# A depthwise convolution moved from VectorE to TensorE, and a longer ring of row tiles, in the first scan of a fused state-space and attention kernel

## The chip, the core and the metric

The kernel runs on one core of a Trainium2 chip. The core has a matrix engine (TensorE, PE in the profile; its weight loads are PEld), a vector engine (VectorE, DVE), an activation engine (ScalarE, ACT), a general engine (GpSimd, POOL) and a queue engine (SyncE, SP) that here issues most of the transfers. The engines run their own instruction streams in order and wait for each other with semaphores. 16 DMA engines carry the transfers. The metric is the device time of one execution in microseconds.

## What is computed

The input x is 32 sequences of 256 tokens with 256 channels. A state-space layer turns it into y, two attention and feed-forward layers follow, and x is added at the end. All is float32. The part that the change touches is the front of the state-space layer (cut to what matters):

```
xr, gate = jnp.split(x @ W_in.T, 2, axis=-1)          # 512 channels each
xr = xr + t_emb[:, None, :]
xc = conv_general_dilated(xr.transpose(0, 2, 1), W_conv, (1,), [(3, 0)],
                          feature_group_count=512) + b_conv   # 4 taps, each channel by itself
xc = silu(xc).transpose(0, 2, 1)
xn = (xc - mean) / sqrt(var + 1e-05) * ln_g + ln_b
Bm, Cm, dt = split(xn @ W_xproj.T, 3, axis=-1)        # 16 states
dt = tanh(dt @ W_dt.T + b_dt) * 0.01
Ad = 1.0 + dt * -tanh(A_log);  Bd = Bm * min(norm(xn), 1.0)
h = clip(h * Ad + Bd * xt, -10, 10);  yt = Ct . h     # a scan over the 256 tokens
y = (ys + D * xn) * silu(gate) @ W_out.T
```

Each token's state h is 16 states by 512 channels per sequence. The convolution is depthwise: an output channel is the sum of four shifted copies of the same input channel, each times a weight of that channel.

## The kernel before

The 32 sequences are four groups of eight (GB). A group's scan holds 8 sequences x 16 states on the 128 partitions and 512 channels along them, so one token of a group is one VectorE instruction of 128x512 (`step`, L718): 256 steps per group, 1024 in all. A token's row of xn has to stand on all 16 states of its sequence, times that state's factor. For most tokens a DMA reads the row from DRAM (tensor xnd) and spreads it over the partitions (`load_rows`, L687, tile xrep); ScalarE multiplies it by the factor (`scale_row`, L708); the step adds it to h. In the first group two tokens of every eight come another way: `load_skip` loads a block of 16 rows (tile xq, L747), and TensorE spreads a row by a product (`spread_rows`, L695, tile bx), which ScalarE scales into a tile of the same ring. Row tiles come from a ring of six (pool xp).

The work of a scan is written as an agenda. Slot s is the step of token s; everything else has a slot relative to it, and a chunk of 32 tokens (CH) starts at slot s0. For the first group (`alone`) the chunk's x is loaded at s0-43; `project` (L401) makes the four blocks of 128 channels from s0-40 on, every second slot; then `conv_in` (s0-38 + 2 ch) puts the 3 tokens carried over from the last chunk (GpSimd, L471 and L473) and the projection plus condition (VectorE, L474) into tile xr, and GpSimd begins the convolution in tile acc with tap 0 and the bias (L480). `conv_taps` one slot later adds taps 1 to 3 on VectorE (L491), and `conv_th` one slot after that takes the Silu on ScalarE (L501). The tiles xr and acc have two buffers each. `raw_sums` (s0-27, L520) and `norm_turn` (s0-26 and s0-22, L550) use the result on TensorE; statistics, scaling and the affine follow, and `norm_out` (s0-17 and s0-13, L593) writes 128 rows each to xnd. `load_skip` reads blocks back at s0-9 and s0+7; `load_rows` of token t stands at slot s0+t-6, and `scale_row` at s0+t-2. Outputs are read from h by TensorE (`read_out`, L730), in groups of four tokens, and gated, turned and projected (L781 to L832). The state tiles h have eight buffers.

During the first scan TensorE also makes the projections of the three other groups, in 48 units (`ahead_project`, L428, 16 records of 256 columns for every two units), which go to DRAM and come back later. The other groups' scans are then interleaved with attention and feed-forward of the groups before; attention starts at slot 274. These groups compute the convolution on GpSimd and VectorE in all versions, with Tanh in place of Silu.

SP's queue holds, in order: row loads, loads of x (L457, L417), blocks xq, writes of xnd, writes of projected tiles (L444), and loads of weights. An instruction in it that waits for a tile to come free holds all that stand behind it. All eight PSUM banks are one pool (psw, tag w) for every kind of product. The order within a slot is first the agenda of the state work and then that of loads and products; from this order and its own estimate of times the framework's planner lays out each engine's stream, and an instruction may be taken ahead of others that wait. Where a tile is given to a new owner, the instruction that first writes it waits for the last owner's users.

The function `program` holds two versions of everything; the data choose the one with `exact` false.

Of the kernel before, what the change touches and what calls it, by code (L numbers as in the profile page):

```python
# [10 lines left out]
FP = mybir.dt.float32  # L11
# [62 lines left out]
def kernel(  # L74
# [149 lines left out]
    def program(ctx, exact):  # L224
# [154 lines left out]
        def group_scan(g):  # L379
# [82 lines left out]
            def conv_in(c, ch):  # L462
                if ch == 0:
                    ck[c]["carry"] = sm.tile(
                        [P, NC_, GB, TAPS - 1], FP, tag="carry", name="carry"
                    )
                    ck[c]["xc"] = sp.tile([P, NC_, GB * CH], FP, tag="xc", name="xc")
                ps = ck[c].pop(("ps", ch))
                xr = sp.tile([P, GB, TAPS - 1 + CH], FP, tag="xr", name="xr", bufs=2)
                if c == 0:  # L470
                    nc.gpsimd.memset(xr[:, :, 0 : TAPS - 1], 0.0)  # L471
                else:
                    nc.gpsimd.tensor_copy(xr[:, :, 0 : TAPS - 1], ck[c - 1]["carry"][:, ch])  # L473
                nc.vector.tensor_add(  # L474
                    xr[:, :, TAPS - 1 :],
                    ps.rearrange("p (b t) -> p b t", b=GB),
                    bc(cond_sb[:, ch, b0 : b0 + GB], 2, CH),
                )
                acc = sp.tile([P, GB, CH], FP, tag="acc", name="acc", bufs=2)
                nc.gpsimd.tensor_scalar(  # L480
                    acc, xr[:, :, 0:CH], wc_sb[:, ch, 0:1], bconv_sb[:, ch : ch + 1],
                    ALU.mult, ALU.add,
                )
                if c < NCH - 1:
                    nc.gpsimd.tensor_copy(ck[c]["carry"][:, ch], xr[:, :, CH:])
                ck[c]["xr", ch] = xr, acc

            def conv_taps(c, ch):
                xr, acc = ck[c]["xr", ch]
# [6 lines left out]
            def conv_th(c, ch):  # L496
                acc = ck[c]["xr", ch][1]
                if alone:

                    ck[c].pop(("xr", ch))  # L500
                    nc.scalar.activation(  # L501
                        ck[c]["xc"][:, ch], acc.rearrange("p b t -> p (b t)"), AF.Silu
                    )
                    return
                th = sp.tile([P, GB * CH], FP, tag="th", name="th", bufs=2)
                nc.scalar.activation(th, acc.rearrange("p b t -> p (b t)"), AF.Tanh, scale=0.5)
                ck[c]["th", ch] = th
# [173 lines left out]
            def by_tensor(t):  # L681
                return alone and t % (2 * NQ) < XR

            def load_rows(c, t):
                xr = xp.tile([P, DI], FP, tag="xrep", name="xrep")
                ck[c]["rep", t] = xr
                nc.sync.dma_start(out=xr, in_=bc(rows(c)[:, t, :], 0, NS))  # L687

# [14 lines left out]

            def scale_row(c, t):
                if by_tensor(t):
                    ck[c]["rep", t] = xp.tile([P, DI], FP, tag="xrep", name="xrep")
                bx = ck[c]["rep", t]
                scaled = nc.scalar.activation(  # L708
                    bx, ck[c].pop(("bx", t), bx), AF.Copy, scale=ck[c]["beta"][:, t : t + 1]
# [140 lines left out]
            rep_w = []  # L850
            at(-1, start)
            if alone:
                at(-30, spread_weights)
                constants(at)
            for c in range(NCH):
# [2 lines left out]
            for c in range(NCH):  # L858
# [7 lines left out]
                    at(s + 11, skip, c, hb)  # L866
                for ch in range(NC_):
                    at(s0 - 38 + 2 * ch, conv_in, c, ch)
                    at(s0 - 37 + 2 * ch, conv_taps, c, ch)
                    at(s0 - 36 + 2 * ch, conv_th, c, ch)  # L870
                    if not alone:
                        at(s0 - 35 + 2 * ch, conv_out, c, ch)
# [24 lines left out]
            for c in range(NCH):  # L897
                s0 = c * CH
                at(s0 - 43 if alone else s0 + 6, load_x, c)
                if alone:  # L900
                    for ch in range(NC_):
                        at(s0 - 40 + 2 * ch, project, c, ch)
                else:
                    for i in range(2):
                        at(s0 - 44 + 2 * i, load_projected, c, i)
# [5 lines left out]
                at(s0 - 8, figures_out, c)  # L911
                for t in range(CH):
                    if not by_tensor(t):
                        at(s0 + t - 6, load_rows, c, t)
                    if by_tensor(t) and t % XR == 0:
                        at(s0 + t - 4, spread_rows, c, t)
                    at(s0 + t - 2, scale_row, c, t)
# [777 lines left out]
```

## Time and profile before

| | us |
|---|---|
| median of 3 runs | 3543.61 (3540.46 to 3543.66) |
| the profiled execution | 3553.66 |
| its span, first to last instruction | 3551.9 |
| busy in the span: TensorE, VectorE, ScalarE, GpSimd | 3441.7, 2605.5, 2037.4, 1620.7 |
| first scan, first step's start to last step's end | 59.2 to 448.7 |

A group line of the profile reads: line of the program, engine, operation, output tile <- input tiles, partitions x elements, count | busy us, mean ns of one | idle time of the engine just before them, and what ended it. A wait line reads: who waited for whom, total us, times, longest. A timeline line reads: start, duration, engine, line, operation, count, and in brackets the idle time before it. Matmuls are pipelined and their ends are modelled, so the time from one start to the next says more of TensorE's pace than its busy time does. One product of float32 operands appears as two records.

### The profile page before, as it was taken

What the parts mean: (1) busy time and instruction counts of PE and PEld (TensorE: products, weight loads), DVE (VectorE), ACT (ScalarE), POOL (GpSimd) and SP (SyncE); (2) the same over time, 40 slices, a digit from 0 to 9 for tenths busy, and PEclk for the clock granted to TensorE, in tenths of its full rate; (3) what the DMA queues carried; (4) which work ended last, traced back from release to release, by engine and by line L of the source; (5) the groups of instructions that cost most, each with busy time, mean ns of one, the idle gap of its engine ahead of it and who ended that gap; (6) DMA issues with size and microseconds to landing.
All of it is one profiled execution on the core that took longest, in us unless ns stands there. A gap on an engine that the chain in (4) does not pass through costs nothing.

```text
span 3551.9 us, 57690 instructions
## 1 busy us (share of the span) xinstructions
PE 3441.7 (97%) x20220; PEld 2263.7 (64%) x20220; DVE 2605.5 (73%) x5049; ACT 2037.4 (57%) x3663; POOL 1620.7 (46%) x1587
## 2 busy tenths in 40 slices
PE   7999989999999999999999999999999999999999
PEld 5445335666666666666666666666666777777777
DVE  4888898877878777877787778787777545555563
ACT  3666656656666656666566656666666444444442
POOL 4433455544545445544454556454443333333441
PEclk8999999999999999999999999999999999999999
DMA  6788765534454555544454445544444212011111
GB/s 183 211 219 217 200 174 153 135 113 134 125 143 138 150 144 150 139 121 126 123 144 131 139 147 146 145 115 129 124 138 118 63 37 62 13 31 35 37 28 38
DMA packets 487199, 436.72 MB, mean 123 GB/s; under 512 B 247155, under 2 KB 326516, under 8 KB 486772
## 3 DMA queue, kind: packets, MB, share of 16 engines
q1 hardware_dynamic: 402450, 420.94, 42.0%
q10 hardware_dynamic: 84450, 12.01, 2.1%
q8 instruction: 162, 2.65, 0.3%
q14 instruction: 137, 1.12, 0.1%
HBM read 384.06 MB, written 47.19 MB: 121 GB/s over the span
## 4 chain that ended last, share of the span: by engine, by line
PE 64%; DVE 16%; DMA 7%; ACT 5%; POOL 4%; issue 3%; SPq 1%; ACTq 0%; DVEq 0%; POOLq 0%
PE ps_qkv L991 13%; PE pa L1402 13%; PE po_f L1429 6%; DVE h L718 6%; DMA xrep<-xnd 5%; PE y L730 5%; PE ps_wo L1047 5%; PE ov L1282 4%; PE ps_in L401 3%; PE ps_out L810 3%; PE sc L1227 3%; PE tr_qk L1036 2%; PE rs L1264 2%; ACT xrep L708 2%; DVE acc L491 2%
## 5 line engine op out<-in xcount | busy, mean ns | idle before, releaser
L718 DVE CUSTOM_DVE_ANT_0 h<-h,xrep,lim 128x512 f32<-128x512 f32 x1024 | 931.9, 910 | 215.1 <-ACT xrep L708 166.5
L708 ACT ACTIVATE xrep<-xrep,beta 128x512 f32<-128x512 f32 x960 | 672.5, 720 | 315.7 <-DMA xrep<-xnd 202.4
L991 PE MATMUL ps_qkv<-qkv,res 128*128 128x512 f32 x1536 | 715.2, 601 | 17.2 <-DVE ag L1420 7.2
L1402 PE MATMUL pa<-hT,w 128*128 128x256 f32 (+1 forms) x2816 | 674.5, 382 | 5.4 <-DVE zT L801 5.1
L1402 PEld LDWEIGHTS pa<-hT,w 128*128 128x128 f32 (+1 forms) x2816 | 517.6, 189 | 145.1 <-issue 38.0
L1015 POOL TENSOR_TENSOR rot<-rot,swp 128x512 f32<-128x512 f32 x256 | 349.0, 1363 | 543.7 <-DVE swp L1012 513.0
L991 PEld LDWEIGHTS ps_qkv<-qkv,res 128*128 128x128 f32 x1536 | 282.2, 191 | 299.8 <-issue 242.2
L1021 POOL TENSOR_TENSOR rn<-ss,neg_half 128x8 f32<-128x8 f32 x256 | 461.0, 1801 | 0.0
L1420 DVE SCALAR_TENSOR_TENSOR ag<-pa,b_sb,ag 128x256 f32<-128x256 f32 x320 | 151.9, 475 | 280.0 <-ACT ag L1413 279.7
L730 PE MATMUL y<-h,ly 128*32 128x512 f32 x2048 | 335.8, 606 | 9.8 <-DVE h L718 9.2
L1429 PE MATMUL po_f<-ag,w 128*128 128x256 f32 x1280 | 305.7, 386 | 1.4 <-DVE fo L1440 0.6
L1354 POOL TENSOR_TENSOR rstd<-ve,neg_half 128x2 f32<-128x2 f32 x64 | 46.1, 720 | 555.9 <-DVE ve L1352 555.9
L1429 PEld LDWEIGHTS po_f<-ag,w 128*128 128x128 f32 x1280 | 235.3, 190 | 64.8 <-DVE xc L511 11.7
L1413 ACT ACTIVATE ag<-pa,b_sb 128x256 f32<-128x256 f32 x320 | 149.9, 469 | 217.8 <-PE pa L1402 215.7
L1004 ACT ACTIVATE sq<-ps_qkv,tiny 128x512 f32<-128x512 f32 x256 | 172.4, 685 | 172.2 <-PE ps_qkv L991 143.8
L1047 PE MATMUL ps_wo<-oT,wo 128*128 128x256 f32 x1024 | 236.2, 385 | 14.2 <-DVE oT L1322 11.2
L1047 PEld LDWEIGHTS ps_wo<-oT,wo 128*128 128x128 f32 x1024 | 196.6, 193 | 45.5 <-issue 9.9
L491 DVE SCALAR_TENSOR_TENSOR acc<-xr,wc_sb,acc 128x256 f32<-128x256 f32 x384 | 188.6, 523 | 46.4 <-POOL acc L480 45.9
L1012 DVE TENSOR_TENSOR swp<-ps_qkv,rs_sb 128x256 f32<-128x256 f32 x512 | 191.8, 416 | 29.8 <-POOL rot L1015 29.6
L1007 DVE TENSOR_TENSOR rot<-ps_qkv,rc_sb 128x512 f32<-128x512 f32 x256 | 173.8, 679 | 45.8 <-ACT sq L1004 45.6
L1239 ACT ACTIVATE pT<-sc 128x512 f32<-128x512 f32 x384 | 202.1, 603 | 7.3 <-PE sc L1227 5.5
L1027 DVE SCALAR_TENSOR_TENSOR rot<-rn,rot 128x512 f32<-128x512 f32 x256 | 196.1, 804 | 5.0 <-POOL rn L1021 4.7
(161 smaller groups left out, 5306.9 us busy)
## 6 DMA issues: line engine op xcount, KB each, us to landing
xrep<-xnd SPq DMA_DIRECT2D x960, 256.0 KB
rb<-inv SPq DMA_DIRECT2D x128, 256.0 KB
xnd<-xn SPq DMA_DIRECT2D x64, 256.0 KB
qkv<-in_wqkv_dram SPq DMA_DIRECT2D x24, 512.0 KB
ahead<-xs_a SPq DMA_DIRECT2D x48, 256.0 KB
xp<-ahead SPq DMA_DIRECT2D x48, 256.0 KB
xd<-xnd SPq DMA_DIRECT2D x192, 64.0 KB
w<-in_w_dram SPq DMA_DIRECT2D x80, 128.0 KB
```

The lines of the kernel that those rows point to most:

```text
L491: nc.vector.scalar_tensor_tensor(acc, xr[:, :, k : k + CH], wc_sb[:, ch, k : k + 1], acc, ALU.mult, ALU.add,)
L708: scaled = nc.scalar.activation(bx, ck[c].pop(("bx", t), bx), AF.Copy, scale=ck[c]["beta"][:, t : t + 1])
L718: nc.vector._custom_dve(TENSOR_ADD_SAT, out=h_new, in0=state["h"], in1=bx, s0=ck[c]["lim"][:, 0, t : t + 1], s1=ck[c]["lim"][:, 1, t : t + 1],
L730: nc.tensor.matmul(ck[c]["y", hb][32 * q : 32 * q + 32, :], ly[hb % 2][:, 32 * t : 32 * t + 32], ck[c].pop(("h", hb * TB + t)), start=(i = ...
L991: nc.tensor.matmul(ps, res[b][:, k, t0 : t0 + W], wt["qkv", a][:, k], start=(k == 0), stop=(k == KM - 1),)
L1015: nc.gpsimd.tensor_add(rot, rot, swp)
L1021: nc.gpsimd.tensor_tensor(rn, ss, neg_half, ALU.pow)
L1027: nc.vector.scalar_tensor_tensor(rot, bc(rn, 2, DH), 1e12, rot, ALU.min, ALU.mult)
L1047: nc.tensor.matmul(po[:, d], wt["wo", 0][:, c, d * P : (d + 1) * P], oT[:, c, :], start=(c == 0), stop=(c == NC_ - 1),)
L1239: nc.scalar.activation(p, banks[r], AF.Exp)
L1402: nc.tensor.matmul(dst[x], wt["w1", m][:, k, x], self.h[:, k], start=(k == 0), stop=(k == KM - 1),)
L1429: nc.tensor.matmul(self.po[:, d], wt["w2", 0][:, m, d * P : (d + 1) * P], self.ag[m], start=(m == 0), stop=(m == len(MCH) - 1),)
```

## The change

In the first scan the convolution's taps become TensorE products: the input block xr, shifted by k tokens, times a 128x128 matrix that has tap k's weights on its diagonal, four products summed in a PSUM bank; ScalarE adds the bias in the Silu and reads the bank. The 16 diagonals are made once, by ScalarE from the identity, in tiles that the attention uses later (tags oT, hn, hT). The ring of row tiles of the first scan grows from six to ten; the four new ones are tiles of the attention (tags qT, kT, rb, v). Its row loads are issued eight slots ahead of the step instead of six.

```diff
                     bc(cond_sb[:, ch, b0 : b0 + GB], 2, CH),
                 )
-                acc = sp.tile([P, GB, CH], FP, tag="acc", name="acc", bufs=2)
-                nc.gpsimd.tensor_scalar(
-                    acc, xr[:, :, 0:CH], wc_sb[:, ch, 0:1], bconv_sb[:, ch : ch + 1],
-                    ALU.mult, ALU.add,
-                )
+                acc = None
+                if not alone:
+                    acc = sp.tile([P, GB, CH], FP, tag="acc", name="acc", bufs=2)
+                    nc.gpsimd.tensor_scalar(
+                        acc, xr[:, :, 0:CH], wc_sb[:, ch, 0:1], bconv_sb[:, ch : ch + 1],
+                        ALU.mult, ALU.add,
+                    )
                 if c < NCH - 1:
                     nc.gpsimd.tensor_copy(ck[c]["carry"][:, ch], xr[:, :, CH:])
                 ck[c]["xr", ch] = xr, acc
+
+            def taps_diagonal(ch):
+                if ch == 0:
+                    t = ap_.tile([P, 2, TAPS, P], FP, tag="oT", name="taps", bufs=1)
+                    state["taps", 0], state["taps", 1] = t[:, 0], t[:, 1]
+                elif ch > 1:
+                    state["taps", ch] = ap_.tile(
+                        [P, TAPS, P], FP, tag=("hn", "hT")[ch - 2], name="taps", bufs=1
+                    )
+                for k in range(TAPS):
+                    nc.scalar.activation(
+                        state["taps", ch][:, k], ident, AF.Copy, scale=wc_sb[:, ch, k : k + 1]
+                    )
+
+            def conv_products(c, ch):
+                xr, _ = ck[c]["xr", ch]
+                ps = bank(ps_w, "w", "cv")[:, 0 : GB * CH]
+                for k in range(TAPS):
+                    nc.tensor.matmul(
+                        ps.rearrange("p (b t) -> p b t", b=GB),
+                        state["taps", ch][:, k],
+                        xr[:, :, k : k + CH],
+                        start=(k == 0),
+                        stop=(k == TAPS - 1),
+                    )
+                ck[c]["xr", ch] = xr, ps
...
                     nc.scalar.activation(
-                        ck[c]["xc"][:, ch], acc.rearrange("p b t -> p (b t)"), AF.Silu
+                        ck[c]["xc"][:, ch], acc, AF.Silu, bias=bconv_sb[:, ch : ch + 1]
                     )
...
+            def row_tile():
+
+                n = state["rows"] = (state.get("rows", -1) + 1) % (6 if exact else 10)
+                if not alone or n < 6:
+                    return xp.tile([P, DI], FP, tag="xrep", name="xrep")
+                tag = ("qT", "kT", "rb", "v")[n - 6]
+                t = ap_.tile(
+                    [P, 2, DI], FP, tag=tag, name="xrep", bufs=2 if tag == "v" else 1
+                )
+                return t[:, 0]
+
             def load_rows(c, t):
-                xr = xp.tile([P, DI], FP, tag="xrep", name="xrep")
+                xr = row_tile()
...
             def scale_row(c, t):
                 if by_tensor(t):
-                    ck[c]["rep", t] = xp.tile([P, DI], FP, tag="xrep", name="xrep")
+                    ck[c]["rep", t] = row_tile()
...
             if alone:
+                for ch in range(NC_):
+                    at(-41 + ch, taps_diagonal, ch)
...
                     at(s0 - 38 + 2 * ch, conv_in, c, ch)
-                    at(s0 - 37 + 2 * ch, conv_taps, c, ch)
+                    if not alone:
+                        at(s0 - 37 + 2 * ch, conv_taps, c, ch)
                     at(s0 - 36 + 2 * ch, conv_th, c, ch)
...
                     for ch in range(NC_):
                         at(s0 - 40 + 2 * ch, project, c, ch)
+                        at(s0 - 37 + 2 * ch, conv_products, c, ch)
...
-                        at(s0 + t - 6, load_rows, c, t)
+                        at(s0 + t - (8 if alone and not exact else 6), load_rows, c, t)
```

## The prediction

> **What bounds the kernel now.** I read the page's head, then windows of one chunk each, the groups and waits of the first scan, and the timelines of TensorE and of SP's queue.
>
> ```profile
> span 3551.9 us, 57690 instructions
> ...
> PE 3441.7 (97%) x20220; PEld 2263.7 (64%) x20220; DVE 2605.5 (73%) x5049; ACT 2037.4 (57%) x3663; POOL 1620.7 (46%) x1587
> ```
> TensorE bounds the whole, but the change touches only the first scan. Its steps (L718) start at 59.2 us and end at 448.7: 389.5 us for 8 chunks of 32 slots, 48.7 us each, 1.52 per slot. Windows of a chunk (PE, PEld, DVE, ACT, POOL busy; clock, DMA share, GB/s):
> ```profile
> 160.00:209.00 49.00, 46.23 (x216) 24.46 (x215) 42.78 (x75) 31.99 (x61) 19.15 (x26) 1.00 0.80 218
> 209.00:258.00 49.00, 45.60 (x189) 24.86 (x192) 41.33 (x74) 29.81 (x55) 18.27 (x25) 0.93 0.84 220
> ...
> 402.00:449.00 47.00, 41.54 (x135) 13.43 (x134) 41.36 (x80) 28.23 (x50) 22.19 (x28) 1.00 0.63 175
> ```
> VectorE has 42 of 49 us, and no engine is full. The groups between 150 and 400 us (5.1 chunks) show what the taps cost:
> ```profile
> L718 DVE CUSTOM_DVE_ANT_0 h<-h,xrep,lim 128x512 f32<-128x512 f32 x164 | 156.6, 955 | 11.5 <-ACT xrep L708 3.5 <-DVE h L718 2.0 <-PE y L730 1.1
> ...
> L491 DVE SCALAR_TENSOR_TENSOR acc<-xr,wc_sb,acc 128x256 f32<-128x256 f32 x65 | 32.8, 505 | 6.2 <-POOL acc L480 6.2
> L480 POOL TENSOR_SCALAR acc<-xr,wc_sb,bconv_sb 128x256 f32<-128x256 f32 x22 | 21.5, 978 | 45.3 <-DVE xr L474 39.4 <-ACT xrep L708 4.0 <-ACT xs_a L439 1.9
> ```
> The waits of the same 250 us (total, times, longest): ScalarE waits for rows, SP's queue for a free row tile (a load needs the step six rows back), and TensorE for the blocks of rows that queue up behind those loads.
> ```profile
> DVE ad L650 <- ACT ad L645: 7.2, 5, 2.0
> ...
> ACT xrep L708 <- DMA xrep<-xnd: 52.6, 44, 3.5
> ...
> PE bx L695 <- DMA xq<-xnd: 7.7, 5, 1.9
> ...
> SPq L687 <- DVE h L718: 35.7, 44, 2.9
> ```
> SP's timeline shows it at a chunk's end: the block is issued at 244.31, after 2.86 us in which a row load waited, and TensorE then idles until 249.67, its first products slow.
> ```profile
> 240.15 2.86 SPq L687 DMA_DIRECT2D xrep<-xnd  x1
> ...
> 244.31 2.64 SPq L747 DMA_DIRECT2D xq<-xnd  x4
> ```
> TensorE's timeline gives its pace, from start to start, since its busy time counts tails:
> ```profile
> 227.82 1.07 PE L730 MATMUL y<-h,ly 128*32 128x512 f32 x8
> ...
> 230.65 1.89 PE L401 MATMUL ps_in<-xg,w_in_sb 128*128 128x256 f32 x8
> ...
> 236.30 1.89 PE L428 MATMUL ps_a<-xa,w_in_sb 128*128 128x256 f32 x8
> 238.12 1.13 PE L695 MATMUL bx<-xq,rep_w 32*128 32x512 f32 x4
> ...
> 249.67 3.11 PE L695 MATMUL bx<-xq,rep_w 32*128 32x512 f32 x4 [2.54 <-ACT xrep L708]
> ```
> Eight records of 256 columns take 1.82 us (236.30 to 238.12), 0.2275 each; each product is two records (16 projections a chunk by the code, 152 records in 5.1 chunks).
>
> **The change, part by part.**
>
> *Taps off VectorE and GpSimd.* Per chunk 12 L491 go. They are 0.505 us each by the group; started back to back in the timeline they advance it by about 0.43, so 5.2 us. The 4 L480 of 0.98 us go too, with VectorE's wait for them, 6.2 / 5.1 = 1.2 us. VectorE falls from 42 to about 37 us of busy time.
>
> *Products onto TensorE.* 4 blocks x 4 taps x 2 records = 32 records x 0.2275 = 7.3 us per chunk. What TensorE already issues per chunk: 104 records of 256 columns (48 L428, 32 L401, 16 L810, 8 L520) 23.7; 16 of L695, four per 1.06 us, 4.2; 64 of L730, eight per 1.00 us, 8.0; 16 transposes 2.0; L620 0.5. Sum 38.4, so 10.3 of the 48.7 us are waits or half clock. After: 45.7. Idle time covers the products, but hardly any is left: **TensorE becomes the bound of the first scan at about 45.7 us per chunk.** The other limits lie lower: VectorE 37, ScalarE 32, DMA 217 GB/s x 48.7 us at a share of 0.80, so 39 us at a share of 1.
>
> *Ring of ten, loads eight slots ahead.* The load now needs the step ten allocations back, two slots done by plan. SP's 35.7 us of waiting for steps should mostly go, and with it what is queued behind: writes of xnd, blocks xq, ahead, xg. Each load is issued two slots (3 us) earlier, with unchanged count and bytes. The first rows of a chunk must follow the write of xnd, but load_skip, one slot earlier in SP's queue, waits for that write already: nothing added. Unless the late block's waits go (7.7 / 5.1 = 1.5 us per chunk, and about as much in half clock), TensorE's 10.3 us of slack isn't usable, so the two parts need each other.
>
> *New waits.* xr has two buffers, now released by TensorE instead of VectorE; conv_in's add stands in VectorE's queue ahead of steps, and a late product holds the steps. Bounds: 0, or three adds a chunk each behind one block's products (1.8 us), 5.5 us. The plan has three slots between, so I take 0.6 with the other residual waits. One more PSUM bank: between 0 and the one bank-like wait shown (L695 behind ACT xrep, 2.5 us in 250), 0.5 per chunk; I take 0. The Silu now reads PSUM; PSUM readers of that size (L474, 0.42) and this row (0.41) differ by nothing.
>
> *Borrowed tiles.* Attention's first use is at slot 274, after the last row's step at 255: 0. Without that cover the first projections would wait a step, 1.5 us.
>
> *Startup.* 16 diagonals on ScalarE: rows of 0.31 (128x32) and 0.41 (128x256) bound them at 5 to 6.6 us; ScalarE is idle 7.3 us there before its first Silu at 17.2, so 0, or 6.6 if they hold the first Silu. Chunk 0's 32 records replace taps that end at 24.9. TensorE's pace there:
> ```profile
> 9.68 5.46 PE L401 MATMUL ps_in<-xg,w_in_sb 128*128 128x256 f32 x12 [9.68 <-DMA xg<-in_xT_dram]
> ...
> 18.02 2.00 PE L428 MATMUL ps_a<-xa,w_in_sb 128*128 128x256 f32 x8
> ...
> 29.66 3.76 PE L428 MATMUL ps_a<-xa,w_in_sb 128*128 128x256 f32 x8
> ```
> At 18 us a record takes 0.24, before 15 and at 30 us 0.45. 32 records are 7.3 to 14.6 us, against about 5 idle us between 15 and 25. [...]
>
> [...]
>
> *Sum.* Chunk with products: 45.7 + 0.6 = 46.3, 2.4 less, in six chunks: 14.4. The last two have no products, only the ring: their floor is VectorE's 41.4 of 47; of 5.6 us I take a third, 1.8 each: 3.6. Startup 0. The attention that follows is TensorE's and unchanged: 0. Together 18 us. The profiled execution took 3553.7 (span 3551.9), 10 above the median of 3543.6; against the median: **3526**. Own range: 3517 to 3536.
>
> **Rivals.**
> - *TensorE too full, slower.* The 10.3 us of waits don't vanish when work is added. If half stay, a chunk takes 45.7 + 5.2 = 50.9: 2.2 more in six, 13; less 3.6; with startup up to 7: 3553 to 3560. It decides from 3.0 us of residual waits per chunk. For: TensorE's order is fixed, and it waits on h, xq and rhs. Against: these waits come from late rows.
> - *Rows are limited by the transfers.* Then the ring only queues them longer: 0 to 1 us per chunk, 3536 to 3550. For: 5 us windows reach a DMA share of 1. Against: 0.8 on the mean, and SP waiting for steps.
> - *More.* At 0.216 per record (chain of waits: eight in 1.73) the floor is 44; with 4.3 in six chunks, 4 in two and 5 at startup: 3505.
> - *The planner's order undoes it* (products late, rows as before): within the second rival.
>
> **How the numbers follow.** No change means within 0.2%, 7 us, about what a measurement tells. Forecast 0.50, more 0.14: faster 0.64. Transfers or order 0.14: same. TensorE 0.22: slower. The range reaches past 3505 by startup's bound, to 3497, and to 3557 in the slower rival.
>
> **What would show it.** Right: chunks of 46 to 47 us, no L491 and L480 ahead of the second group's convolution, VectorE near 37 per chunk, SP's waits for h nearly gone, ACT's for rows halved, TensorE's start-to-start sum 45 to 46 per chunk at full clock. Wrong: chunks over 48.7; VectorE's L474 waiting for the products; L695 still waiting for xq; the DMA share at 1; a first step later than 59.2 us; or any change in time after 449 us, which nothing here explains.

## The result and the profile after

The changed kernel took 3579.21 us (median of 5, 3576.81 to 3583.29) against 3543.61 for the kernel before: a ratio of 1.010, 95% interval 1.0088 to 1.0112. It is **36 us slower**. The forecast was 3526 us, so the sign was wrong. The rival that had TensorE too full had the sign but gave 3553 to 3560.

The profiled execution took 3582.63 us. These are the span and the busy times of its page.

```profile
span 3580.8 us, 58077 instructions
...
PE 3464.5 (97%) x20476; PEld 2294.1 (64%) x20476; DVE 2552.2 (71%) x4953; ACT 2045.0 (57%) x3679; POOL 1601.5 (45%) x1555
```

The step is now L757 and the row load L726. The first scan runs from 55.1 to 475.7 us, 420.6 us of steps. Before it was 389.5, and 391.7 in another profiled execution of the kernel before (3544.93 us). After the last step of the first scan 3105.2 us remain, against 3103.2 and 3104.1. So 29 to 31 us of the 36 come from the steps of the first scan, and nothing from what follows it. By chunk, from first step to first step (the last one to the first step of the second group), in us:

| chunk | 0 | 1 | 2 | 3 | 4 | 5 | 6 | 7 |
|---|---|---|---|---|---|---|---|---|
| before | 52.0 | 48.8 | 48.9 | 49.9 | 48.4 | 48.2 | 47.5 | 46.6 |
| after | 53.1 | 51.0 | 53.1 | 51.5 | 54.2 | 57.4 | 54.8 | 46.2 |

"A chunk" below is the mean of chunks 1 to 5: 48.8 before (48.9 in the other execution), 53.4 after. These are the windows of the changed kernel over the stretches shown of before (PE, PEld, DVE, ACT, POOL busy; clock, DMA share, GB/s).

```profile
160.00:209.00 49.00, 43.40 (x217) 26.48 (x216) 30.97 (x54) 28.33 (x53) 14.26 (x17) 1.00 0.73 198
209.00:258.00 49.00, 44.88 (x223) 27.13 (x222) 34.34 (x58) 30.95 (x57) 16.46 (x21) 0.97 0.71 191
402.00:449.00 47.00, 42.93 (x155) 16.42 (x156) 38.85 (x75) 25.27 (x46) 19.41 (x26) 0.96 0.61 188
```

VectorE is relieved, 31 and 34 of 49 us where it had 43 and 41, and TensorE, ScalarE and GpSimd are busy for no more of the time than before. The DMA share fell from 0.80 and 0.84 to 0.73 and 0.71. So no engine has taken over as one that is always at work: they wait for each other. Two groups of 150 to 400 us, the step and the new products:

```profile
L757 DVE CUSTOM_DVE_ANT_0 h<-h,xrep,lim 128x512 f32<-128x512 f32 x149 | 130.1, 873 | 61.5 <-ACT xrep L747 40.8 <-PE y L769 13.0 <-DVE h L757 1.2
...
L507 PE MATMUL cv<-xr,taps 128*128 128x256 f32 x160 | 40.1, 393 | 5.6 <-DVE xr L474 4.3 <-DVE ad L678 1.3
```
The waits of the same 250 us on ScalarE and TensorE (total, times, longest):
```profile
ACT xrep L747 <- DMA xrep<-xnd: 79.6, 44, 6.3
...
PE ps_raw L548 <- ACT xc L529: 5.4, 4, 2.2
...
PE cv L507 <- DVE xr L474: 4.3, 3, 2.3
```
And those of SP's queue:
```profile
SPq L726 <- DVE h L757: 36.8, 45, 3.7
SPq L444 <- ACT xs_a L439: 31.6, 14, 5.2
SPq L621 <- POOL xn L617: 24.8, 9, 4.2
```

The steps idle 61.5 us (11.5 before), ScalarE waits 79.6 us for rows (52.6 before), and SP still waits as long for steps (36.8; 35.7 before). Which rows the steps wait for is told by the tile bx, the rows that TensorE spreads. Among those who waited for an instruction on bx that ran in these 250 us (total, times), the step stands as follows, first in the changed kernel, then in the kernel before:
```profile
  DVE h L757: 44.7, 14
```
```profile
  DVE h L718: 0.2, 1
```
In the other execution of the kernel before it is 1.4 us. So the steps' new waits for ScalarE are for TensorE's rows, not for loaded ones. In the changed kernel ScalarE scales, in chunks 1 to 5, 4.0 loaded rows of later tokens on the mean ahead of the first TensorE row of eight tokens (0.1 before), and any of them can make it wait for a transfer.

The timelines at 269 to 280 us show how one wait makes the next. SP's queue:

```profile
272.60 1.04 SPq L726 DMA_DIRECT2D xrep<-xnd  x1
278.89 0.34 SPq L444 DMA_DIRECT2D ahead<-xs_a  x1
279.29 4.21 SPq L726 DMA_DIRECT2D xrep<-xnd  x5
```
ScalarE:
```profile
275.97 0.72 ACT L747 ACTIVATE xrep<-xrep,beta 128x512 f32<-128x512 f32 x1 [3.08 <-DMA xrep<-xnd]
277.31 0.72 ACT L747 ACTIVATE xrep<-xrep,beta 128x512 f32<-128x512 f32 x1 [0.62 <-DMA xrep<-xnd]
277.94 0.46 ACT L529 ACTIVATE xc<-cv,bconv_sb 128x256 f32<-128x256 f32 x1
278.30 0.57 ACT L439 COPY xs_a<-ps_a 128x512 f32<-128x512 f32 x1
278.76 1.28 ACT L747 ACTIVATE xrep<-bx,beta 128x512 f32<-128x512 f32 x2
```
TensorE:
```profile
269.02 2.00 PE L507 MATMUL cv<-xr,taps 128*128 128x256 f32 x8
270.86 1.89 PE L428 MATMUL ps_a<-xa,w_in_sb 128*128 128x256 f32 x8
272.67 1.13 PE L734 MATMUL bx<-xq,rep_w 32*128 32x512 f32 x4
273.73 1.06 PE L769 MATMUL y<-h,ly 128*32 128x512 f32 x8
274.73 1.51 PE L548 MATMUL ps_raw<-xc,wx_sb 128*64 128x256 f32 x6
278.45 0.65 PE L548 MATMUL ps_raw<-xc,wx_sb 128*64 128x256 f32 x2 [2.21 <-ACT xc L529]
```
VectorE:
```profile
279.50 0.81 DVE L757 CUSTOM_DVE_ANT_0 h<-h,xrep,lim 128x512 f32<-128x512 f32 x1 [6.09 <-ACT xrep L747]
```

The last convolution product is done by 270.9. Its Silu (L529) stands in ScalarE's queue behind the scaling of rows that arrive late, so it ends at 278.4, and TensorE waits 2.21 us for it. The copy of projected tiles (L439) stands behind it, SP's put of that copy waits until 278.89, and five row loads wait behind the put. VectorE's next step waits 6.09 us meanwhile, for a row that TensorE has spread by 273.73 and that ScalarE scales only behind all this, from 278.76. Which link of this chain costs time is what the experiments ask.

### The profile page after: what moved, and what is told of

Its sections match the earlier page's. It is cut to its first block, busy times and chain, and to the rows that moved or that the text cites. A ratio compares the mean times of both kernels' runs of the same rounds, so it can differ in the third digit from the quotient of the medians.

```text
span 3580.8 us, 58077 instructions
## 1 busy us (share of the span) xinstructions
PE 3464.5 (97%) x20476; PEld 2294.1 (64%) x20476; DVE 2552.2 (71%) x4953; ACT 2045.0 (57%) x3679; POOL 1601.5 (45%) x1555
## 4 chain that ended last, share of the span: by engine, by line
PE 61%; DVE 17%; DMA 8%; ACT 6%; POOL 5%; issue 3%; SPq 1%; ACTq 0%; DVEq 0%; POOLq 0%
PE ps_qkv L1034 13%; PE pa L1445 13%; DVE h L757 6%; DMA xrep<-xnd 6%; PE po_f L1472 6%; PE ps_wo L1090 5%; PE ov L1325 4%; PE y L769 3%; PE sc L1270 3%; PE ps_in L401 2%; PE ps_out L849 2%; PE tr_qk L1079 2%; ACT xrep L747 2%; PE rs L1307 2%; DVE acc L519 2%
## 5 line engine op out<-in xcount | busy, mean ns | idle before, releaser
L757 DVE CUSTOM_DVE_ANT_0 h<-h,xrep,lim 128x512 f32<-128x512 f32 x1024 | 921.2, 900 | 277.5 <-ACT xrep L747 209.3
L769 PE MATMUL y<-h,ly 128*32 128x512 f32 x2048 | 319.2, 610 | 8.6 <-DVE h L757 8.0
L1397 POOL TENSOR_TENSOR rstd<-ve,neg_half 128x2 f32<-128x2 f32 x64 | 46.2, 722 | 557.0 <-DVE ve L1395 556.9
L1270 PE MATMUL sc<-qT,kT 64*64 64x192 f32 (+2 forms) x2816 | 187.5, 322 | 0.0
```

The costliest lines, as they stand in the source:

```text
L757: nc.vector._custom_dve(TENSOR_ADD_SAT, out=h_new, in0=state["h"], in1=bx, s0=ck[c]["lim"][:, 0, t : t + 1], s1=ck[c]["lim"][:, 1, t : t + 1],
L769: nc.tensor.matmul(ck[c]["y", hb][32 * q : 32 * q + 32, :], ly[hb % 2][:, 32 * t : 32 * t + 32], ck[c].pop(("h", hb * TB + t)), start=(i = ...
L1270: nc.tensor.matmul(banks[r][k0 : k0 + mk, i, q0:q1], kT[rows, i0 + i, kw * W + k0 : kw * W + k0 + mk], qT[rows, i0 + i, kw * W + q0 : kw * ...
```

## The experiments

Theories. **W**, work: TensorE has less room than the sum of the forecast says, and any records added to it cost time. **L**, lateness: the convolution's result comes later than it did from VectorE, and what needs it is late. **Q**, queue: SP's queue is blocked by the puts of L444, now that TensorE is later. Against all of these stood the **ring**: the loss could be that of more loads issued earlier. A letter in an expectation stands for the theory that it tests; the first ones call W by the letter F and the ring R, and T is the rows' transfers. In the tables "chunk" is the mean of chunks 1 to 5 in the profiled execution, and the ratio is to the kernel before, with its 95% interval.

### The two parts, and the queue

Products alone: the changed kernel with the ring and the lead as before.
```diff
-                n = state["rows"] = (state.get("rows", -1) + 1) % (6 if exact else 10)
+                n = state["rows"] = (state.get("rows", -1) + 1) % 6
...
-                        at(s0 + t - (8 if alone and not exact else 6), load_rows, c, t)
+                        at(s0 + t - 6, load_rows, c, t)
```


> The convolution by TensorE's products alone; the ring stays at six tiles and the loads six slots ahead. Three theories of the loss of 36 us. F (TensorE too full): the products' 32 records a chunk are the loss, whatever the ring: 3570 to 3595 us. Q (SP's queue): the projected tiles' puts and the writes of xnd stand in SP's queue ahead of row loads and wait for ScalarE and GpSimd, which the products made late; the shorter ring can only make it worse: 3575 to 3600. R (the ring): ten tiles and the longer lead bunch the transfers, and the products are harmless: 3520 to 3545.

Ring alone: the kernel before with `row_tile` and the lead of eight.
```diff
-                xr = xp.tile([P, DI], FP, tag="xrep", name="xrep")
+                xr = row_tile()
...
-                        at(s0 + t - 6, load_rows, c, t)
+                        at(s0 + t - (8 if alone and not exact else 6), load_rows, c, t)
```


> The ring of ten and the lead of eight slots alone; the convolution stays on VectorE and GpSimd. F and Q: the ring takes waits away and adds none, 3520 to 3542 us. R: about as slow as the whole change, 3565 to 3580.

The puts of projected tiles moved from SP's queue to ScalarE's:
```diff
-                nc.sync.dma_start(out=d, in_=state.pop(("ta", u)))
+                nc.scalar.dma_start(out=d, in_=state.pop(("ta", u)))
```


> The whole change, but the puts of the projected tiles (L444) are issued from ScalarE's queue, directly behind the copy that they wait for, so that no row load stands behind them in SP's queue. Q: SP waited 31.6 us for these copies in 250 us, 6.2 per chunk; most of the loss goes, 3545 to 3562 us. F and R: no more than 5 us better, 3573 to 3582.

One product of four for each block, the other three taps left out:
```diff
-                for k in range(TAPS):
+                for k in range(1):
...
-                        state["taps", ch][:, k],
-                        xr[:, :, k : k + CH],
+                        state["taps", ch][:, 3],
+                        xr[:, :, 3 : 3 + CH],
```


> The whole change with one product per block in place of four: taps 0 to 2 of the first group's convolution are left out, so TensorE has 8 records more per chunk than before instead of 32, and everything else (banks, tiles, who waits for whom) is as in the whole change. F: 5.5 us a chunk come back, 3530 to 3548. Q: the producers are early again, 3535 to 3560. R: 3570 to 3580.

| | median us | before | ratio | chunk |
|---|---|---|---|---|
| products alone | 3582.62 | 3544.28 | 1.0114 (1.0095 to 1.0133) | 53.2 |
| ring alone | 3548.08 | 3544.28 | 1.0015 (1.0004 to 1.0027) | 49.4 |
| puts on ScalarE's queue | 3577.55 | 3544.28 | 1.0092 (1.0075 to 1.0110) | 52.5 |
| one tap of four | 3540.03 | 3544.28 | 0.9983 (0.9973 to 0.9992) | 49.1 |

The products are the whole loss; the ring neither helps nor hurts by more than 0.3%. It did lift waits, but no gain came with it. SP's waits of the ring alone, 110 to 360 us:
```profile
SPq L724 <- DVE h L755: 14.4, 28, 1.3
```
The kernel before, over the same stretch of its other execution:
```profile
SPq L687 <- DVE h L718: 27.7, 39, 1.8
```
Half of SP's waiting for steps went, and a chunk is 49.4 us instead of 48.9. Q falls as the main cause: the put that blocks SP in the timeline above is off its queue, and 0.9 us of a chunk's 4.6 goes. With three of four products left out the loss is gone but no gain appears, although VectorE has lost its taps.

One more profiled execution of the kernel before serves as a second row for comparisons:

> The kernel before once more, for a second profile. The first one took 10 us more than the median; if startup is where executions differ, its first step starts near 50 us in place of 59.2 and the chunks are the same 48 to 49 us.

It took 3544.93 us, with its first step at 47.3 us (59.2 in the first profile) and 48.9 us a chunk (48.8).

### Work or lateness

The changed kernel with half of the products of `ahead_project` left out; the convolution stays where it is:
```diff
-                    for k in range(KM):
+                    for k in range(1):
...
-                            start=(k == 0),
-                            stop=(k == KM - 1),
+                            start=True,
+                            stop=True,
```


> The whole change with one of the two products of each projection made ahead for the other groups; half of that projection's sum is left out. TensorE issues 24 records a chunk less (5.5 us), so 8 more than before instead of 32; the convolution is the whole change's, at its place. W: 3535 to 3552 us. L: the convolution ends where it did, 3565 to 3580.

The same edit in the kernel before:

> The kernel before with the same half of the ahead projections left out: 24 records a chunk less and nothing else. It says whether TensorE's work was already felt before. If its waits were only those of rows and steps (the prediction's reading): 3538 to 3546 us. If TensorE's queue already set part of the pace: 3505 to 3530.

The kernel before with four products more for each block, which nobody reads, in the slot where the change has its own:
```diff
+            def extra(c, ch):
+                ps = bank(ps_w, "w", "ex")[:, 0 : GB * CH]
+                for k in range(TAPS):
+                    nc.tensor.matmul(
+                        ps,
+                        ident,
+                        w_in_sb[:, 0, k * GB * CH : (k + 1) * GB * CH],
...
+                        at(s0 - 37 + 2 * ch, extra, c, ch)
```


> The kernel before with the four products of each block added and used by nobody: constant operands, one bank, no wait but for the bank; the taps stay on VectorE and GpSimd. It is the price of 32 records a chunk off any chain. W: as much as the change lost or more, since VectorE keeps its taps, 3575 to 3600 us. L: the planner puts them where TensorE waits anyway, 3545 to 3560.

The changed kernel with the load of x, its projection, `conv_in`, the products and the Silu six slots earlier:
```diff
-                    at(s0 - 38 + 2 * ch, conv_in, c, ch)
+                    at(s0 - (44 if alone else 38) + 2 * ch, conv_in, c, ch)
...
-                        at(s0 - 37 + 2 * ch, conv_products, c, ch)
+                        at(s0 - 43 + 2 * ch, conv_products, c, ch)
```


> The whole change with the first group's load of x, projection, products and Silu six slots earlier in the agenda. Two theories are left, both with the products as the cause. L (lateness): the products end a chunk's convolution about four slots later than the taps did, the planner's orders of SP, ScalarE and GpSimd assume it earlier, and the queues stand at its consumers (norm, writes of xnd) with row loads behind them; six slots give this back: 3540 to 3558 us. W (work): TensorE's records by themselves, wherever they stand: 3573 to 3585.

| | median us | before | ratio | chunk |
|---|---|---|---|---|
| half of the ahead products, changed kernel | 3547.48 | 3551.21 | 0.9989 (0.9979 to 0.9999) | 49.0 |
| half of the ahead products, kernel before | 3559.96 | 3551.21 | 1.0027 (1.0014 to 1.0039) | 51.1 |
| unused products added to the kernel before | 3593.02 | 3551.21 | 1.0123 (1.0106 to 1.0139) | 55.5 |
| convolution six slots earlier | 3609.25 | 3551.21 | 1.0165 (1.0148 to 1.0182) | 58.0 |

W stands: 32 records that nobody waits for cost the kernel before 6.7 us a chunk (7.3 us at their own pace), and taking 24 others away gives the change's whole loss back with the convolution as late as it was: a chunk's last Silu ends 24 steps ahead of the chunk in both, 27 in the kernel before. So L is not needed. The change's 4.6 us a chunk can then be read as 6.7 for the records, less about 2 for the taps that leave VectorE and GpSimd; no run measures these 2.

One rival stands beside W. The framework's planner lays out every engine's stream anew for each edit. With the unused products ScalarE scales 1.9 rows of later tokens ahead of TensorE's row (0.1 before), and in 150 to 400 us the steps wait 16.9 us for that row (0.2 before). How much of the 6.7 us is the records' own time and how much this order was not separated.

The run with everything six slots earlier does not bear on L. In it `ps_in` takes 17.96 us a chunk from start to start (9.23 in the changed kernel): it moved a wait of its own into the chunk. The author's reading is that the projection waits there for x, whose two buffers are still held by the gate's projection.

Nor does the kernel before gain when its TensorE is lighter (51.1 us, and 3559.96). TensorE was no limit of the kernel before by itself. Why that run is 9 us slower is not settled.

### Rows

The changed kernel with the odd ones of the loaded rows not loaded; ScalarE scales the row before it in their place, so all scalings and steps remain:
```diff
+            def shared(t):
+                return alone and not by_tensor(t) and t % 2 == 1
...
-                if by_tensor(t):
+                if by_tensor(t) or shared(t):
...
-                    bx, ck[c].pop(("bx", t), bx), AF.Copy, scale=ck[c]["beta"][:, t : t + 1]
+                    bx,
+                    ck[c]["rep", t - 1] if shared(t) else ck[c].pop(("bx", t), bx),
+                    AF.Copy, scale=ck[c]["beta"][:, t : t + 1]
...
-                    if not by_tensor(t):
+                    if not by_tensor(t) and not shared(t):
```


> The whole change, with the three odd rows of every eight that a transfer brings left out: ScalarE scales the row before once more into a tile of its own, so 12 of 24 row loads a chunk go (3.1 of 10.6 MB) and nothing else; the first group's scan runs on wrong rows. W (TensorE's added records set the chunk of 53 us): within 8 us of the whole change, 3572 to 3590. T (what is left of the bound is the rows' transfers, which the products only disturb): 3530 to 3555.

The same edit in the kernel before:

> The kernel before with the same 12 row loads a chunk left out in the same way. Taking 24 records from TensorE gained nothing before. If the rows' transfers set the chunk of 48.7 us: 45 us or less, 3505 to 3530. If neither does by itself and the queues hold each other: 3535 to 3552.

The changed kernel with xr and the diagonals in bf16, so that a product is one record instead of two (its windows of 110 to 360 us hold 1138 of TensorE's records, 223 in a chunk of 49.1 us; the changed kernel's trace has 236 a chunk):
```diff
-                xr = sp.tile([P, GB, TAPS - 1 + CH], FP, tag="xr", name="xr", bufs=2)
+                xr = sp.tile([P, GB, TAPS - 1 + CH], BF if alone else FP, tag="xr", name="xr", bufs=2)
...
-                    t = ap_.tile([P, 2, TAPS, P], FP, tag="oT", name="taps", bufs=1)
+                    t = ap_.tile([P, 2, TAPS, P], BF, tag="oT", name="taps", bufs=1)
```


> The whole change with the convolution's input and the diagonals in bfloat16, so that a product is one record instead of two: the four products are kept, at a lower precision of the first group's convolution. TensorE then issues 16 short records a chunk more than before, in place of 32. W: nearly all of the loss comes back, 3535 to 3555. If the products' place in the chain were the loss, the records' number would not matter: 3565 to 3580.

Both of these edits in the changed kernel:

> The products in bfloat16 and the three odd loaded rows of every eight left out, both as in the runs before. VectorE is free of the taps and TensorE has 16 short records more than before; by itself each of the two edits left a chunk at about 49 to 50 us. If three limits lie side by side near 49 us (VectorE's stream with the taps, TensorE's with the products, the rows' transfers), this lifts all three: 44 to 46 us a chunk, 3505 to 3525. If the planner's orders or the queues set 49 us whatever the work: 3535 to 3550.

Half of the rows and half of the ahead products, in the changed kernel:

> The whole change in float32 with half of the loaded rows and half of the ahead projections' products left out, both as in the runs before: TensorE has 8 records a chunk more than the kernel before, the transfers 70% of it, VectorE no taps. Side by side limits: 44 to 46 us a chunk, 3505 to 3525. Queues alone: 3535 to 3550.

| | median us | before | ratio | chunk |
|---|---|---|---|---|
| changed kernel, half rows | 3554.97 | 3544.21 | 1.0027 (1.0015 to 1.0040) | 50.0 |
| kernel before, half rows | 3541.59 | 3544.21 | 0.9989 (0.9979 to 0.9999) | 48.7 |
| bf16 products | 3543.27 | 3544.21 | 0.9999 (0.9990 to 1.0009) | 49.1 |
| bf16 products, half rows | 3533.13 | 3550.19 | 0.9955 (0.9940 to 0.9971) | 46.1 |
| half rows, half ahead | 3534.53 | 3550.19 | 0.9957 (0.9939 to 0.9974) | 47.3 |

The first of these speaks against W alone, which wanted 3572 us or more: the records cost what they do together with the loading of rows. The last two are slower than the 3505 to 3525 us that were expected of them.

Four of these make a square: taps on VectorE or as cheap products, rows all loaded or half. Its lower line has the ring of ten too, which by itself left a chunk at 49.4.

| us per chunk | all rows | half rows |
|---|---|---|
| taps on VectorE | 48.8 | 48.7 |
| taps as bf16 products | 49.1 | 46.1 |

Each alone gives nothing, both together 2.7 us. So two limits stand side by side at about 49 us in the kernel before: VectorE with its taps, and the loading of rows. The rows' limit is seen with bf16 products, in windows and waits of 110 to 310 us: VectorE and TensorE both have room, the DMA share rises to 0.87, ScalarE waits for loaded rows, and the steps wait for rows that ScalarE scales. By the tile bx all of these 24.5 us are for TensorE's rows, scaled behind loaded ones.
```profile
210.00:260.00 50.00, 44.48 (x226) 25.69 (x223) 35.96 (x65) 30.67 (x58) 16.23 (x22) 0.96 0.87 221
```
```profile
ACT xrep L748 <- DMA xrep<-xnd: 40.2, 31, 3.3
DVE h L758 <- ACT xrep L748: 24.5, 10, 4.6
```
The other limit is seen in the kernel before with half of the rows. VectorE is busy 43.95 of 50 us (last line, the mean over four windows), the steps no longer wait for rows (0.8 us in 200), and what it waits for are answers to its own work:
```profile
210.00:260.00 50.00, 47.13 (x209) 24.15 (x209) 43.56 (x77) 32.45 (x60) 20.40 (x26) 1.00 0.56 144
260.00:310.00 50.00, 47.90 (x214) 24.82 (x211) 44.31 (x75) 33.31 (x62) 21.09 (x27) 1.00 0.57 149
sum 200.00, PE 190.17 PEld 98.10 DVE 175.81 ACT 131.10 POOL 84.39; mean PE 47.54 PEld 24.52 DVE 43.95 ACT 32.77 POOL 21.10
```
```profile
DVE ad L650 <- ACT ad L645: 7.4, 4, 2.2
DVE st L560 <- PE tp_x L550: 6.3, 5, 1.5
DVE acc L491 <- POOL acc L480: 3.6, 12, 0.3
...
DVE h L723 <- ACT xrep L711: 0.8, 4, 0.3
```

### Lighter rows for good

In the next three the first group's rows are stored, loaded and spread in bf16, into six raw tiles loaded six slots ahead; ScalarE scales each into one of eight float32 tiles, which `row_tile` now gives. Everything is computed, with fewer bits. The core of the edit, against the changed kernel:
```diff
-                ck[c]["xnd"] = dp.tile([GB * CH, DI], FP, tag="xnd", name="xnd")
+                ck[c]["xnd"] = dp.tile(
+                    [GB * CH, DI], BF if alone else FP, tag="xnd0" if alone else "xnd", name="xnd"
+                )
...
-                xr = row_tile()
+                xr = xp.tile([P, DI], BF if alone else FP, tag="xrep", name="xrep")
...
-                if by_tensor(t):
+                src = ck[c].pop(("bx", t)) if by_tensor(t) else ck[c]["rep", t]
+                if alone:
                     ck[c]["rep", t] = row_tile()
...
-                    xd = ap_.tile([P, HEADS, DH], FP, tag="rot", name="xq", bufs=4)
+                    xd = ap_.tile([P, HEADS, DH], BF, tag="rot", name="xq", bufs=4)
...
-                t = aw.tile([P, NI, NS, GB], FP, tag="pT", name="rep_w", bufs=6)
+                t = aw.tile([P, NI, NS, GB], BF, tag="pT", name="rep_w", bufs=6)
```
With bf16 products:

> A version that computes everything: products in bfloat16, and the first group's rows stored, loaded and spread in bfloat16 (128 KB a load in place of 256), six tiles for loaded rows and eight for scaled ones. Precision of the first group is lower. Side by side limits: 3505 to 3528. Queues alone: 3535 to 3555.

With the change's float32 products:

> The whole change's float32 products with the rows of the first group in bfloat16, as in the last version. TensorE keeps the 32 records; the rows no longer press. If TensorE's own floor with the products is 47 to 50 us a chunk: 3535 to 3555. If the products only hurt because rows were short: as good as with bfloat16 products, 3505 to 3515.

With the taps on GpSimd and VectorE as before the change:

> Rows of the first group in bfloat16, the taps on VectorE and GpSimd as before the change. If VectorE's stream with the taps is the bound of the kernel before: a chunk stays at 47.5 to 49 us, 3533 to 3550. If the rows were it: 3505 to 3520.

| bf16 rows with | median us | before | ratio | chunk |
|---|---|---|---|---|
| bf16 products | 3506.18 | 3550.19 | 0.9871 (0.9852 to 0.9890) | 42.7 |
| float32 products | 3532.74 | 3550.59 | 0.9947 (0.9926 to 0.9967) | 45.9 |
| taps on VectorE | 3524.93 | 3550.59 | 0.9920 (0.9897 to 0.9944) | 45.2 |

The first beats both kernels, by 1.3% against the kernel before. With rows out of the way the other two show each engine near its own limit. With float32 products it is TensorE, in windows of 110 to 310 us:
```profile
110.00:160.00 50.00, 49.56 (x268) 31.90 (x264) 40.35 (x65) 33.70 (x64) 20.54 (x26) 1.00 0.56 145
160.00:210.00 50.00, 47.52 (x246) 31.04 (x246) 42.42 (x75) 33.82 (x64) 17.05 (x23) 1.00 0.61 150
...
sum 200.00, PE 193.33 PEld 124.13 DVE 164.51 ACT 136.24 POOL 75.36; mean PE 48.33 PEld 31.03 DVE 41.13 ACT 34.06 POOL 18.84
```
With the taps on VectorE it is VectorE:
```profile
160.00:210.00 50.00, 48.80 (x234) 27.30 (x236) 46.82 (x82) 35.01 (x67) 20.66 (x27) 1.00 0.59 150
210.00:260.00 50.00, 48.24 (x230) 26.24 (x222) 47.11 (x79) 36.47 (x71) 21.39 (x27) 1.00 0.59 142
...
sum 200.00, PE 191.13 PEld 104.28 DVE 187.10 ACT 141.05 POOL 89.13; mean PE 47.78 PEld 26.07 DVE 46.77 ACT 35.26 POOL 22.28
```
TensorE's busy time hardly differs in the two (48.33 and 47.78 of 50 us), since its ends are modelled; from start to start its read-outs take 8.3 us a chunk in the first and 15.2 in the second. Each limit gives way when its engine is relieved: with bf16 products a chunk is 42.7 us, 3.2 and 2.5 us less.

Both runs came out faster than expected. With float32 products a chunk is 45.9 us where 47 to 50 were expected. With the taps on VectorE it is 45.2 where 47.5 to 49 were expected. The latter expectation took VectorE with its waits as the bound of the kernel before at 48.7 us whatever the rows do. But bf16 rows also make L695's spreading one record instead of two (34 records in 200 us with float32 products, 8 a chunk, where the changed kernel has 16; 1.3 us a chunk, where the kernel before with half of the rows has 4.2), and VectorE waits less for the transposes of TensorE (1.3 us in 200, where `st` waits 6.3 above). So a part of that 48.7 probably came from TensorE. In these three runs a loaded row's tile also comes free when it is scaled, not when it is stepped; that was not tried by itself.

## Why the prediction was wrong

**The step that failed: "10.3 of the 48.7 us are waits or half clock", and what followed, "45.7" and "0.6 ... residual waits".** This is TensorE's time in a chunk (mean of chunks 1 to 5), counted over the trace's records from one start to the next, so that a wait is charged to the kind ahead of it:

| us per chunk | forecast | before | after | float32 products, bf16 rows |
|---|---|---|---|---|
| the convolution's products | 7.3 | | 7.6 | 7.4 |
| 104 records of L428, L401, L520, L810 | 23.7 | 27.9 | 28.1 | 25.3 |
| read-outs L730 | 8.0 | 11.0 | 8.3 | 8.3 |
| spreading L695 | 4.2 | 7.1 | 5.3 | 1.3 |
| transposes and L620 | 2.5 | 2.9 | 4.1 | 3.5 |
| sum | 45.7 | 48.9 | 53.4 | 45.9 |

Three things are to be read in it.

1. The products cost what was forecast: 7.6 us against 7.3.
2. The work of the others was sized a little too low. The last column is TensorE with the least idle time (1.5 us a chunk by the modelled ends), and the kinds that it shares with the forecast, without the spreading, take 37.1 us there, where the forecast had 34.2. About half of the difference is that idle time. Group by group the prices agree: eight records of 256 columns advance TensorE by 1.82 us at the median, the change to the next kind included, and eight read-outs by 1.00. With the spreading of float32 rows at 4.2 (the forecast, and what the kernel before with half of the rows has) in place of 1.3, the last column gives an estimate of TensorE's need for the change: 48.8 us with its idle time, 47.3 without. So the floor was 1.6 us higher than 45.7, and under the kernel before's chunk of 48.8 there was room for some 1.5 us, and for that only if every wait went.
3. **The waits did not go**, and this is most of the miss. Of what TensorE waited in the kernel before, the products absorbed 2.7 us at the read-outs, 1.8 at the spreading and 0.9 at L428. New waits came at the sums L520 (1.1 us more, the wait for the Silu), at the transposes (0.9) and at L620 (0.3). 53.4 is 6.1 above 47.3, where the forecast had left 0.6. Halving the row loads gives 3.4 of the 6.1 back, so more than half goes with the loading of rows. The timeline of 269 to 280 us shows one way from late rows to TensorE, through ScalarE's queue; that it is the main one was not tried. The condition of the rival that had TensorE too full ("3.0 us of residual waits") was met: it let half of the 10.3 us stay, and 7.7 did, 53.4 being that far above 45.7.

**The second step that failed: "VectorE has 42 of 49 us, and no engine is full", and the ring that was to lift the waits.** Of the parts of the change, none gained alone: the ring took half of SP's waits for steps away and a chunk stayed at 49.4, taps that cost TensorE half as much left it at 49.1, a lighter TensorE at 51.1, half of the rows at 48.7. The forecast took a chunk at 48.7 us with no full engine for a chunk with slack. It was one with several limits close to each other, VectorE with the round trips of its work and the loading of rows among them. So the rival that rows are limited by the transfers came near what the chunk is once TensorE has room (49.1 us with bf16 products), which is not the case that the change is, and whether transfers or queues hold the rows there was not separated.

Point by point, for the rest:

- *Taps off VectorE and GpSimd*: right. VectorE's busy time is 33 of 49 us in the two windows, about 36 a chunk of 53.4, where 37 was forecast.
- *Blocks late*: right in itself. TensorE's wait of L695 for xq, 7.7 us in 250, is gone, and no gain came with it. The wait at 249.67 that the prediction put down to the late block ended, by its own line, with a scaling on ScalarE.
- *SP's waits for steps mostly gone*: wrong in the whole change (36.8 us in 250; 35.7 before). The ring does let a load be issued further ahead, 9.2 steps before its own step instead of 5.3 (means of chunks 1 to 5), and its scaling starts 5.8 us after the issue instead of 5.3. So loaded rows were ready early, and the steps waited for TensorE's rows, scaled behind them.
- *New waits*: the release of xr by TensorE was costed within 0.6 us. It shows: GpSimd's copy of the carry waits 18.1 us in 250 for the products, and TensorE waits 4.3 for the add of `conv_in`. The transfer of the wait to VectorE's L474 did not come (it waits 2.3 for the projection, none for the products).
- *The last two chunks*: wrong in chunk 6. "No products" held by plan for three quarters of chunk 7's blocks; 23 of 32 records ran in chunk 6, which took 54.8 us instead of 47.5. The records there explain 5.2 us. But chunk 6 is long, 51.6 to 57.5 us, in all kernels that have the convolution on TensorE with float32 rows or float32 products, even in that with one tap (52.5), but for the one with the convolution six slots earlier (49.5); why is open.
- *Startup*: the 16 diagonals take 4.8 us on ScalarE, 0.3 each. Chunk 0's four groups of products advance TensorE by 2.23, 1.74, 1.82 and 1.83 us, so all but the first ran at 0.22 to 0.23 us a record, as in the steady chunks. No run shows the 5 us gained or the 7 and 8 us lost at startup that the rivals and the range contain. What the runs show is where the first step comes, at 55.1 us, and at 59.2 and 47.3 in the two executions of the kernel before, and TensorE's clock and pace ahead of it. In the first of these two the granted clock was 0.50 from 25.2 to 49.1 us, and eight records of L428 at 29.66 took 3.76 us; in the second eight of them at 27.03 took 1.97, with no products added; in the changed kernel the clock was 0.50 between 15 us and the first step only from 38.3 to 45.1. The rest of the 36 us, 5 to 7, lies here by subtraction, but first steps scatter so between executions that no run assigns it.
- *The profiled execution of before, "10 above the median"*: the other execution shows that these 10 us lay ahead of the first step (59.2 against 47.3).
- *After the first scan nothing*: right, 3103.2 and 3105.2 us.
- *More, from a floor of 44 at 0.216 us a record*: the same fault as the forecast. The pace is right within a group (0.216 us from one record to the next at the median, in both kernels), but the waits stayed.
- *The clock*: not the cause. Stretches with a granted clock of 0.50 fell from 4.8 us a chunk (3.4 in the other execution) to 2.7.
- *The range*: its lower end counts startup twice. 3505 holds 5 us gained at startup, and 3497 takes 8 more off for startup's bound. Its upper end, 3557, stops short of the 3560 of the slower rival.

The busy share of TensorE's weight loads (PEld) tells the same when it is read against a run instead of as a share of 100: in the run above with the least idle TensorE it is 31.03 of 50 us, 62%; in the kernel before 24.7 of 49, 50%. Scaled by the first, the change's 29.2 us of weight loads in a chunk (26.8 of 49, in a chunk of 53.4) would need 47 us, an estimate that agrees with the 47.3 above. With such a run at hand, this row would have told that the products leave little room.

What stays open: which of the limits of the kernel before binds first at which moment of a chunk; why the kernel before gets slower with fewer ahead products; what the planner's order of ScalarE's stream costs, since no run kept the order and changed the work; and chunk 6. That the rows' limit lies in the transfers rather than in the order of SP's and ScalarE's queues was not separated: halving the loads lightens both.

## What to carry to other kernels

An engine's idle time need not be room for more work: its waits can stay, and new ones come, when work is added (here 10.3 us of 48.7 seemed free, and 32 unused records cost 6.7). Try it first with unused work on that engine, which costs a run and no design. When a stage runs at a steady pace and no engine is full, look for several limits at the same height before moving work from one to another; take work off each of them in turn and off two at once, since it can take a pair to show it (48.7 and 49.1 us a chunk alone, 46.1 together). An in-order queue that mixes late inputs (rows for later steps) with results that others wait for (a Silu, the row of the next step) can hand lateness on to them (here 2.21 us to TensorE and 6.09 to a step).

## What was not expected of the hardware

- 32 records that nothing waits for, on an engine whose records seemed to leave 10.3 us of 48.7 free, cost 6.7 us a chunk: nearly their whole 7.3.
- Rows that TensorE had spread in time held the steps for 44.7 us in 250 (0.2 before), while ScalarE scaled loaded rows of later tokens ahead of them, 4.0 on the mean, and waited for their transfers.
- Lightening one thing at a time left a chunk where it was (ring, rows, bf16 products: 49.4, 48.7, 49.1 us against 48.8), rows and bf16 products together took 2.7 us off it (46.1), and bf16 rows with bf16 products 6.1 (42.7).
